# A four-layer graph network on one core: layer 2's mask codes loaded in half quarters, its elu split over ScalarE, GpSimd and VectorE

## The chip, the core and the metric

The kernel runs on one core of a Trainium2 chip. The metric is device time in microseconds (us) for one execution. The core's engines are called here as in the profile: PE (TensorE, matrix products; PEld is its weight load), DVE (VectorE), ACT (ScalarE), POOL (GpSimd) and SP (SyncE, which here only issues DMAs). Each engine runs its own instructions in order, and waits on semaphores for the others. SBUF is the on-chip memory with 128 partitions, PSUM the memory into which PE accumulates.

## The reference

4096 nodes with 256 features go through four layers, each of the form x = x + f(relu(layernorm(x)), adj) with one adjacency matrix of 4096 x 4096. Layer 0 is a graph attention with several gated branches, layer 1 a mean over neighbours, layer 3 a masked self attention. The change concerns layer 2 and the bias of layer 1:

```python
def _L1_gnn_ref(x, adj, W, b):
    a = (adj == 1).astype(x.dtype)
    deg = jnp.sum(a, axis=1, keepdims=True)
    agg = jnp.einsum('ij,jf->if', a, x) / deg
    return agg @ W.T + b

def _L2_gnn_ref(x, adj, W, a):
    ...
    h = x @ W
    e_src = h @ a[:D, 0]
    e_dst = h @ a[D:, 0]
    e = e_src[:, None] + e_dst[None, :]
    e = jnp.where(e > 0, e, NEG_SLOPE * e)
    att_logits = jnp.where(adj > 0, e, MASK_VAL)
    attention = jax.nn.softmax(att_logits, axis=1)
    h_prime = attention @ h
    return jax.nn.elu(h_prime)

h = jnp.maximum(_layernorm(x, axis=-1), 0.0)
x = x + _L1_gnn_ref(h, adj, L1_gnn_W, L1_gnn_b)
h = jnp.maximum(_layernorm(x, axis=-1), 0.0)
x = x + _L2_gnn_ref(h, adj, L2_gnn_W, L2_gnn_a)
```

## The kernel before

All rows of x stay in SBUF in the tile `xs`, as 32 row tiles of 128 rows by 256 features. Layer 0 has turned the adjacency matrix into a mask in bf16 (the "turned codes"), transposed so that the neighbour lies on the partition, and stored it in device memory as `codesT`: for each of 8 blocks of 4 row tiles, four quarters of 1 MB, a quarter holding 8 of the 32 chunks of 128 neighbours. In each partition a quarter is one run of 8 KB.

Layer 2 is an object of the class `Attention` (`att2`), which layer 0 uses too. It goes through the 8 blocks, and in each block through 16 pairs of chunks (128 pairs in all). For one pair:

- DVE computes two logits `y` (L354, one for each chunk, 128 x 512), from `ab_row` (the terms of the row nodes, spread over all partitions), `cdst` (the term of the neighbour) and `b` (a copy of half of `ab_row`, L352, made once a block).
- POOL subtracts the mask (L358, 128 x 1024, both chunks at once). The turned codes are its second operand.
- ACT takes the exponential of each chunk (L386), which also adds the neighbour's term.
- PE multiplies (L407): 4 row tiles by 2 chunks, each with 257 columns, the first column of ones giving the softmax's denominator. Four accumulators `acc` in PSUM collect the block; the pool has five.

There are 8 buffers for `y`, and PE is issued 3 pairs behind DVE.

The softmax needs a bound for each row, and that is what `reach` (L289 for a block's first chunk, L291 for the others) computes ahead: DVE keeps the running extreme `run` over all 32 chunks of a block, from the same turned codes. It runs 16 + 7 pairs ahead of the pairs that PE consumes (LEAD is 7), so during block b it finishes block b+1 and begins block b+2. When a block's run is complete, `top` follows in steps: PE transposes the run (L311), DVE reduces it and forms `ab` (L315 to L320), PE transposes `ab` (L323), ACT copies it and issues a DMA that stores it (`l_ab_d`, L340) and then one that loads it spread over all partitions (`ab_row`, L342). These two DMAs are on ACT's queue, among the exponentials. The next block's copy of `b` waits for `ab_row`.

The turned codes of layer 2 come through `stored` (L944 to L948): the first request for a quarter takes a buffer of the pool `l2_turned` and issues the load on SP. The pool has 8 buffers, two blocks' worth. So quarter q of block b+2 takes the buffer of quarter q of block b, and SP's issue waits until POOL's subtraction on the last pair of that quarter (pairs 3, 7, 11 and 15) has read it. The first of DVE's runs that needs the new quarter waits for the load. In blocks 0 to 5 codes for a later block are loaded; blocks 6 and 7 load nothing and have no runs of a block after next.

The order of instructions on each engine isn't the order of the program's text: the framework's scheduler moves them when the kernel is built, and places the runs of `reach` earlier than written, where it holds that their codes will have come. On the chip each engine follows that order.

At the end of a block `run` takes the reciprocals of the denominators (`rden`, L416), one for each row tile, and calls `finish2` (L953 to L970), which computes x + elu(h) for the block's four row tiles. With h = acc * rden, it uses elu(h) = max(h, 0) + min(exp(h), 1) - 1, written as max(h - 1, -1) + min(exp(h - 1 + 1), 1):

- `hp` = acc * rden - 1, row tiles 0 and 2 on ACT (L963, with `minus` as its bias), 1 and 3 on DVE (L959);
- `e` = exp(hp + 1), one operation of 128 x 1024 on ACT (L967);
- DVE: e = min(e, 1) + rows of x (L969), then rows = max(hp, -1) + e (L970), each 128 x 1024.

Layer 1 adds its bias `b1`, which `load_row` brings into SBUF spread over all partitions, through POOL's DMA queue, at the start of layer 1. POOL's queue at that place goes on with statistics of the layer norm (L117) and loads of adjacency (L173). Layer 2's first step is a layer norm of `xs`, which takes away any constant added to a row. Layer 3 follows layer 2 and reads `xs` row tile by row tile: statistics, layer norm, projections.

Of the kernel before, what the change touches and what calls it, by code (L numbers as in the profile page):

```python
# [11 lines left out]
F32 = mybir.dt.float32  # L12
# [9 lines left out]
P = 128  # L22
# [19 lines left out]
def kernel(ctx: ExitStack, tc: tile.TileContext, w: dict, out: bass.AP):  # L42
# [49 lines left out]
    def load_matrix(pool, name, eng=None):  # L92
        src = w[name]
        k, m = src.shape[0] // P, src.shape[1]
        t = pool.tile([P, k, m], F32, name=f"w_{name}")
        (eng or nc.gpsimd).dma_start(out=t, in_=src.rearrange("(k p) m -> p k m", p=P))
        return t
# [94 lines left out]
    class Attention:  # L192
        def __init__(self, es, tag, slope, lag, n_y, blocks, turned, finish, ps_top=None):
            self.tag, self.slope, self.lag, self.n_y = tag, slope, lag, n_y
            self.turned, self.finish = turned, finish

            self.links = []
            self.blocks = [{"at": at, "n": n} for at, n in blocks]
            vp = es.enter_context(tc.tile_pool(name=f"{tag}_sd", bufs=1))
            self.sdst = vp.tile([P, NT], F32, name="sdst")  # L200
            self.cdst = vp.tile([P, NT], F32, name="cdst")
            self.own_dst, self.held = None, False
            self.ab_d = [
                dram.tile([2, n, P], F32, name=f"{tag}_ab_d{k}") for k, (_, n) in enumerate(blocks)
            ]
            self.picks, self.spread = None, 0
            self.small = es.enter_context(tc.tile_pool(name=f"{tag}_small", bufs=4))
            self.row_p = es.enter_context(tc.tile_pool(name=f"{tag}_rows", bufs=2))
            self.ps_run = es.enter_context(tc.tile_pool(name=f"{tag}_run", bufs=1, space=PSUM))
            self.ps_top = ps_top or es.enter_context(  # L210
                tc.tile_pool(name=f"{tag}_top", bufs=1, space=PSUM)
            )
# [59 lines left out]
        def reach(self, n):  # L272

            b, c = n // PPB, n % PPB * 2
            st = self.blocks[b]
            at, n = st["at"], st["n"]
            if c == 0:
                st["run"] = self.ps_run.tile([P, RB, P], F32, tag="run", name="run")[:, 0:n, :]  # L280
            for j in range(c, c + 2):
                code = self.turned(b, j // QT)[:, :, j % QT, :]
                dst = self.dst_of(slice(j, j + 1))
                to = st["run"]
                if j == NT - 1:
                    to = self.row_p.tile([P, RB, P], F32, tag="run", name="run_sb", bufs=1)
                    to = to[:, 0:n, :]
                if j == 0:
                    nc.vector.tensor_scalar(to, code, dst, None, ALU.subtract)  # L289
                else:  # L290
                    nc.vector.scalar_tensor_tensor(  # L291
                        to, code, dst, st["run"], ALU.subtract, ALU.min
                    )
                st["run"] = to
            if c == NT - 2 and not self.held:
                self.links.append(self.top(b))
                if b == 0:
                    self.top_now()
# [48 lines left out]
        def logits(self, y, b, c, mask):  # L347

            st = self.blocks[b]
            if c == 0:  # L350
                st["b"] = self.ps_b.tile([P, RB, P], F32, tag="b", name="b")[:, 0 : st["n"], :]
                nc.vector.tensor_copy(st["b"], st["ab"][:, 1, :, :])  # L352
            for k in range(2):
                nc.vector.scalar_tensor_tensor(  # L354
                    y[:, :, k, :], st["ab"][:, 0, :, :], self.cdst[:, c + k : c + k + 1],
                    st["b"], ALU.add, ALU.max,
                )
            nc.gpsimd.tensor_tensor(y, y, mask[:, :, c % QT : c % QT + 2, :], ALU.subtract)  # L358

        def run(self, es, lead, n_acc, ahead=lambda n: None):  # L360

# [11 lines left out]
            for n in range(len(pairs) + LAG):  # L373
                if n < len(pairs):
                    b, c = pairs[n]
                    ahead(n)
                    if n + PPB + lead < len(pairs):
                        self.reach(n + PPB + lead)
                    y = self.y_p.tile([P, RB, 2, P], F32, tag="y", name="y")
                    ys[n] = y = y[:, 0 : self.blocks[b]["n"], :, :]  # L380
                    self.logits(y, b, c, self.turned(b, c // QT))
                if n >= LAG:
                    b, c = pairs[n - LAG]
                    y = ys.pop(n - LAG)
                    for k in range(2):
                        nc.scalar.activation(  # L386
                            y[:, :, k, :], y[:, :, k, :], AF.Exp,
                            bias=self.sdst[:, c + k : c + k + 1],
                        )
                    if c == 0:  # L390
                        accs[b] = [
                            ps_acc.tile([P, D + 1], F32, tag="acc", name="acc")
                            for _ in range(self.blocks[b]["n"])
                        ]


                    held.append((c, y))
                    edge = NT - 2 - c < 4 or b > 0 and c < 4
                    if edge and len(held) < 2:
                        self.link()  # L400
                        continue
                    terms = [(r, c1 + k, y1) for r in range(len(accs[b]))
                             for c1, y1 in held for k in range(2)]
                    if not edge:
                        terms.sort(key=lambda term: term[1])
                    for r, j, y1 in terms:
                        nc.tensor.matmul(  # L407
                            out=accs[b][r], lhsT=y1[:, r, j % 2, :], rhs=self.v[:, j, 0 : D + 1],
                            start=(j == 0), stop=(j == NT - 1),
                        )  # L410
                    held.clear()
                    if c == NT - 2:
                        done = accs.pop(b)
                        rden = self.small.tile([P, RB], F32, tag="rden", name="rden")
                        for r, acc in enumerate(done):
                            nc.vector.reciprocal(rden[:, r : r + 1], acc[:, 0:1])  # L416
                        self.finish(self.blocks[b]["at"], done, rden)
                self.link()
# [522 lines left out]
    l2 = ctx.enter_context(ExitStack())  # L941
    loaded = {}

    def stored(b, q):  # L944
        if (b, q) not in loaded:
            loaded[b, q] = turned_p.tile([P, RB, QT, P], BF16, tag="turned", name="turned")
            nc.sync.dma_start(out=loaded[b, q], in_=codesT[b][q])
        return loaded[b, q]  # L948

    minus = const.tile([P, 1], F32, name="minus")  # L950
    nc.gpsimd.memset(minus, -1.0)

    def finish2(at, accs, rden):  # L953

        h = work2.tile([P, RB, D], F32, tag="hp", name="hp")
        for r, acc in enumerate(accs):
            by = rden[:, r : r + 1]
            if r % 2:
                nc.vector.tensor_scalar(  # L959
                    h[:, r, :], acc[:, 1 : D + 1], by, -1.0, ALU.mult, ALU.add  # L960
                )
            else:
                nc.scalar.activation(  # L963
                    h[:, r, :], acc[:, 1 : D + 1], AF.Identity, scale=by, bias=minus
                )
        e = work2.tile([P, RB, D], F32, tag="e", name="e")
        nc.scalar.activation(e, h, AF.Exp, bias=ones[:, 0:1])  # L967
        rows = xs[:, at : at + RB, :]
        nc.vector.scalar_tensor_tensor(e, e, 1.0, rows, ALU.min, ALU.add)  # L969
        nc.vector.scalar_tensor_tensor(rows, h, -1.0, e, ALU.max, ALU.add)  # L970

    cuts2 = [(t, RB) for t in range(0, NT, RB)]
    att2 = Attention(l2, "l2", 0.01, 3, 8, cuts2, None, finish2)
# [19 lines left out]
    with ExitStack() as es:  # L993
# [3 lines left out]
        over_a = es.enter_context(tc.tile_pool(name="l1_a", bufs=AHEAD))  # L997
        vp = es.enter_context(tc.tile_pool(name="l1_v", bufs=1))
        w1 = load_matrix(vp, "L1_gnn_WT")
        b1 = load_row(vp, "L1_gnn_b")  # L1000
        late1 = vp.tile([P, NB - EARLY, BT, 2, D], F32R, name="late1")
        v1 = [t[:, b, :, :, :] for t in (early1[0], late1) for b in range(t.shape[1])]
        work = es.enter_context(tc.tile_pool(name="l1_work", bufs=2))
# [124 lines left out]

    with ExitStack() as es:
        att2.hold(es)  # L1130
        turned_p = es.enter_context(tc.tile_pool(name="l2_turned", bufs=8))
        work2 = es.enter_context(tc.tile_pool(name="l2_work", bufs=1))
        att2.turned, att2.held = stored, False
        with ExitStack() as ps_:
            pst = ps_.enter_context(tc.tile_pool(name="l2_pst", bufs=3, space=PSUM))
            psm = ps_.enter_context(tc.tile_pool(name="l2_psm", bufs=3, space=PSUM))
# [252 lines left out]
```

## Time and profile before

| | us |
|---|---|
| runs | 2970.71, 2976.31, 2978.07 |
| median | 2976.31 |
| the profiled execution | 2973.7 |
| its span in the profile | 2971.9 |
| granted PE clock, mean | 0.988 of full speed |

The profile is of one execution. Its page has the busy time of each engine, groups of instructions by line (busy time, mean of one in ns, idle time of the engine before them and what ended it), and the DMA issues. In the groups `out<-in` are the program's names of tiles. Layer 2's pairs run from 1509.28 to 1999.08 us of the span; layer 1 begins at about 1200, layer 3's matmuls over the scores at 2043.69. Some rows that the reader needs:

| line, engine | what | mean of one |
|---|---|---|
| L354, DVE | logits y, 128x512 | 0.74 us (one starts 0.66 after the one before) |
| L291, DVE | run, 128x512 | 0.75 us (0.79 apart when one needs the one before) |
| L358, POOL | mask, 128x1024 | 2.16 us (2.10 apart) |
| L386, ACT | exponential, 128x512 | 0.71 us |
| L963, ACT | hp of one row tile | 0.56 us |
| L967, ACT | e, 128x1024 | 1.15 us |
| L959, DVE | hp of one row tile | 0.48 us |
| L969, DVE | e, 128x1024 | 1.22 us (last block) to 1.71 |
| L970, DVE | rows, 128x1024 | 1.22 us (last block) to 2.49 |
| L947, SP | load of a quarter, 1 MB, 8 KB runs | 4.8 us from issue to landing (median) |

A duration is from an instruction's start to its end; the engines overlap one instruction's end with the next one's start, so the distance between starts is what a chain of them costs. Where an engine idles, the profile names the event that ended the wait; a wait for several things is put down to the one that came last.

### The profile page before, as it was taken

The numbers are of one execution on the slowest core, as the hardware profiler recorded it, in microseconds if no ns is written. First come the engines' busy times: TensorE is split into PE (matmuls) and PEld (weight loads), VectorE is DVE, ScalarE is ACT, GpSimd is POOL, SyncE is SP. The second block draws the span as 40 slices with busy tenths as digits, with TensorE's granted clock in tenths as the row PEclk, the third lists the DMA queues.
The fourth block names the chain that finished last, engine by engine and source line by source line (L and its number), as shares of the span: only waits on it lengthen the run. The fifth ranks groups of instructions, "written<-read, shape, count | busy, mean of one in ns | idle before, by whom it ended". The sixth has DMA issues, their size and how long they took to land.

```text
span 2971.9 us, 35206 instructions
## 1 busy us (share of the span) xinstructions
PE 2864.4 (96%) x13381; PEld 2336.5 (79%) x13381; DVE 1901.4 (64%) x3475; ACT 1262.0 (42%) x1929; POOL 952.2 (32%) x718
## 2 busy tenths in 40 slices
PE   7999999999999999899999999999999999999999
PEld 6888888856555666788778777888888888888888
DVE  6987767345555554577688888656766666566653
ACT  6765555389995333881354333343111112111111
POOL 5676665545554333320055555550000000000000
PEclk9999999999999999999999999999999999999999
DMA  6966664154551000785432212002111111111100
GB/s 155 235 141 142 133 125 127 43 87 77 78 77 34 8 8 15 190 226 156 140 129 79 75 68 78 29 14 87 37 62 36 38 36 60 40 34 63 34 8 8
DMA packets 109161, 238.62 MB, mean 80 GB/s; under 512 B 10736, under 2 KB 31200, under 8 KB 100288
## 3 DMA queue, kind: packets, MB, share of 16 engines
q1 hardware_dynamic: 68496, 159.34, 15.5%
q0 software_dynamic: 37696, 69.11, 15.1%
q10 hardware_dynamic: 2800, 7.92, 0.7%
q8 instruction: 105, 1.72, 0.2%
q14 instruction: 64, 0.52, 0.1%
HBM read 265.63 MB, written 37.81 MB: 102 GB/s over the span
## 4 chain that ended last, share of the span: by engine, by line
PE 64%; DVE 9%; ACT 8%; POOL 7%; issue 6%; DMA 6%; POOLq 0%; ACTq 0%; DVEq 0%
PE acc L1321 15%; PE s L154 15%; PE acc L407 13%; PE mm L154 9%; PE acc L1052 8%; POOL y L358 5%; ACT sign L180 3%; DVE y L354 3%; DVE run L291 3%; DMA turned<-codesT 2%; DMA ab_row<-l_ab_d 1%; DMA a<-in_adj_dram 1%; PE q_ps L154 1%; DMA l_ab_d<-abT_sb 1%; PE cT L530 1%
## 5 line engine op out<-in xcount | busy, mean ns | idle before, releaser
L407 PE MATMUL acc<-v,y 128*128 128x257 f32 x4096 | 930.2, 386 | 12.3 <-ACT hp L963 4.9
L407 PEld LDWEIGHTS acc<-v,y 128*128 128x128 f32 x4096 | 778.1, 192 | 126.5 <-ACT hp L963 6.5
L358 POOL TENSOR_TENSOR y<-y,turned 128x1024 f32<-128x1024 f32 (+1 forms) x272 | 549.1, 2039 | 323.8 <-DVE y L354 222.3
L386 ACT ACTIVATE y<-y,sdst 128x512 f32<-128x512 f32 (+1 forms) x544 | 350.3, 690 | 417.8 <-POOL y L358 417.6
L1321 PE MATMUL acc<-v,y 128*128 128x257 f32 x2048 | 454.5, 380 | 0.4 <-DVE rden L1329 0.4
L154 PE MATMUL s<-qT,hT 128*128 128x256 f32 x2048 | 445.2, 379 | 0.7 <-ACT qT L1269 0.7
L1314 ACT ACTIVATE y<-y 128x1024 f32<-128x1024 f32 x128 | 132.2, 1055 | 714.3 <-DVE y L1313 710.0
L154 PEld LDWEIGHTS s<-qT,hT 128*128 128x128 f32 x2048 | 389.0, 190 | 54.2 <-ACT qT L1269 1.4
L1321 PEld LDWEIGHTS acc<-v,y 128*128 128x128 f32 x2048 | 387.1, 190 | 55.9 <-issue 0.8
L354 DVE SCALAR_TENSOR_TENSOR y<-ab_row,cdst,b 128x512 f32<-128x512 f32 (+1 forms) x544 | 366.2, 709 | 62.9 <-PE acc L407 61.0
L180 ACT ACTIVATE sign<-a,limits 128x1024 bf16<-128x1024 bf16 x256 | 293.8, 1148 | 22.1 <-DMA a<-in_adj_dram 16.8
L1283 DVE SCALAR_TENSOR_TENSOR y<-code,s 128x512 f32<-128x512 bf16 x256 | 175.9, 688 | 100.9 <-PE s L154 100.6
L291 DVE SCALAR_TENSOR_TENSOR run<-turned,v,run 128x512 f32<-128x512 bf16 (+1 forms) x270 | 186.4, 690 | 63.9 <-ACT turned L535 55.6
L291 DVE SCALAR_TENSOR_TENSOR run<-turned,dst,run 128x512 f32<-128x512 bf16 x240 | 180.5, 752 | 33.1 <-DMA turned<-codesT 29.6
L1313 DVE TENSOR_TENSOR y<-y,top 128x1024 f32<-128x1024 f32 x128 | 146.2, 1215 | 43.0 <-PE top L1307 43.0
L1290 DVE TENSOR_TENSOR mx<-mx,y 128x512 f32<-128x512 f32 x224 | 154.8, 691 | 7.4
L535 ACT ACTIVATE turned<-cT,log_wide 128x1024 bf16<-128x1024 bf16 x128 | 139.0, 1104 | 39.8 <-PE cT L530 31.5
L154 PE MATMUL mm<-kept 128*128 128x512 f32 x288 | 136.7, 615 | 3.0 <-ACT sz L840 1.9
L173 POOL DMA_DIRECT2D a<-in_adj_dram x128 | 76.6, 600 | 196.3 <-ACT sign L180 141.1
L1052 PE MATMUL acc<-early,eq 128*128 128x512 f32 x512 | 128.7, 401 | 2.5 <-DVE early L456 2.2
L1052 PE MATMUL acc<-late,eq 128*128 128x512 f32 x512 | 122.6, 391 | 0.0
L1052 PEld LDWEIGHTS acc<-early,eq 128*128 128x128 f32 x512 | 96.8, 191 | 26.8 <-DVE early L456 2.4
(234 smaller groups left out, 3005.5 us busy)
## 6 DMA issues: line engine op xcount, KB each, us to landing
turned<-codesT SPq DMA_DIRECT2D x36, 1024.0 KB, 4.9
adj_t<-in_adj_dram POOLq DMA_DIRECT2D x128, 256.0 KB, 6.1
codesT<-turned SPq DMA_DIRECT2D x32, 1024.0 KB, 4.9
a<-in_adj_dram POOLq DMA_DIRECT2D x128, 256.0 KB, 4.7
code<-codesT SPq DMA_DIRECT2D x128, 256.0 KB, 4.8
code<-codesT SPq DMA_DIRECT2D x64, 512.0 KB, 7.1
ab_row<-l_ab_d ACTq DMA_DIRECT2D x14, 512.0 KB, 3.8
xs<-in_x_dram SPq DMA_DIRECT2D x8, 512.0 KB, 13.4
```

The costliest lines, as they stand in the source:

```text
L154: nc.tensor.matmul(out=ps, lhsT=lhsT_of(k), rhs=rhs_of(k), start=(k == 0), stop=(k == n - 1))
L180: nc.scalar.activation(sign, self.came[g], AF.Sign, bias=limits[:, v : v + 1], accum_out=over[:, t, v, q : q + 1],)
L291: nc.vector.scalar_tensor_tensor(to, code, dst, st["run"], ALU.subtract, ALU.min)
L354: nc.vector.scalar_tensor_tensor(y[:, :, k, :], st["ab"][:, 0, :, :], self.cdst[:, c + k : c + k + 1], st["b"], ALU.add, ALU.max,)
L358: nc.gpsimd.tensor_tensor(y, y, mask[:, :, c % QT : c % QT + 2, :], ALU.subtract)
L386: nc.scalar.activation(y[:, :, k, :], y[:, :, k, :], AF.Exp, bias=self.sdst[:, c + k : c + k + 1],)
L407: nc.tensor.matmul(out=accs[b][r], lhsT=y1[:, r, j % 2, :], rhs=self.v[:, j, 0 : D + 1], start=(j == 0), stop=(j == NT - 1),)
L1052: nc.tensor.matmul(out=acc, lhsT=eqs[c // (NT // 2)][:, ts(c % (NT // 2), P)], rhs=v1[c // BT][:, c % BT, :, :], start=(c == 0), stop=(c = ...
L1283: nc.vector.scalar_tensor_tensor(y[:, :, c : c + 2, :], st["code"][:, :, c : c + 2, :], -BIG / UNIT, ps, ALU.mult, ALU.add,)
L1290: nc.vector.tensor_tensor(mx, mx, y[:, :, c : c + 2, :], ALU.max)
L1313: nc.vector.tensor_tensor(part, part, top, ALU.subtract)
L1321: nc.tensor.matmul(out=accs[r], lhsT=st["y"][:, r, c, :], rhs=v3[:, c, :], start=(c == 0), stop=(c == NT - 1),)
```

## The change

Three things are changed together.

- Layer 2's turned codes are loaded in half quarters: 4 chunks (two pairs), 512 KB, in each partition 4 runs of 1 KB. The pool has 16 buffers of half the size, so the same memory. `per` (chunks in one load) takes the place of `QT` in the class; in layer 0 it stays QT. There are 64 loads on SP for 32. A half's buffer comes free after POOL's subtraction on its second pair.
- `finish2` computes elu(h) + x as relu(h) + min(exp(h), 1) + (x - 1). On ACT two operations for each row tile, straight from PSUM: relu(acc * rden) to `h` and exp(acc * rden) to `e`. Then POOL adds `h` to the rows (128 x 1024), and one DVE operation gives rows = min(e, 1) + rows. In the last block POOL isn't used: DVE does both, one row tile at a time.
- The rows hold x - 1 during layer 2: POOL subtracts 1 from layer 1's bias right after its load. The tile `minus` goes.

```diff
--- before.py
+++ after.py
@@ -193,6 +193,7 @@
         def __init__(self, es, tag, slope, lag, n_y, blocks, turned, finish, ps_top=None):
             self.tag, self.slope, self.lag, self.n_y = tag, slope, lag, n_y
             self.turned, self.finish = turned, finish
+            self.per = QT
 
             self.links = []
             self.blocks = [{"at": at, "n": n} for at, n in blocks]
@@ -279,7 +280,7 @@
             if c == 0:
                 st["run"] = self.ps_run.tile([P, RB, P], F32, tag="run", name="run")[:, 0:n, :]
             for j in range(c, c + 2):
-                code = self.turned(b, j // QT)[:, :, j % QT, :]
+                code = self.turned(b, j // self.per)[:, :, j % self.per, :]
                 dst = self.dst_of(slice(j, j + 1))
                 to = st["run"]
                 if j == NT - 1:
@@ -355,7 +356,8 @@
                     y[:, :, k, :], st["ab"][:, 0, :, :], self.cdst[:, c + k : c + k + 1],
                     st["b"], ALU.add, ALU.max,
                 )
-            nc.gpsimd.tensor_tensor(y, y, mask[:, :, c % QT : c % QT + 2, :], ALU.subtract)
+            at = c % self.per
+            nc.gpsimd.tensor_tensor(y, y, mask[:, :, at : at + 2, :], ALU.subtract)
 
         def run(self, es, lead, n_acc, ahead=lambda n: None):
 
@@ -378,7 +380,7 @@
                         self.reach(n + PPB + lead)
                     y = self.y_p.tile([P, RB, 2, P], F32, tag="y", name="y")
                     ys[n] = y = y[:, 0 : self.blocks[b]["n"], :, :]
-                    self.logits(y, b, c, self.turned(b, c // QT))
+                    self.logits(y, b, c, self.turned(b, c // self.per))
                 if n >= LAG:
                     b, c = pairs[n - LAG]
                     y = ys.pop(n - LAG)
@@ -941,33 +943,33 @@
     l2 = ctx.enter_context(ExitStack())
     loaded = {}
 
-    def stored(b, q):
-        if (b, q) not in loaded:
-            loaded[b, q] = turned_p.tile([P, RB, QT, P], BF16, tag="turned", name="turned")
-            nc.sync.dma_start(out=loaded[b, q], in_=codesT[b][q])
-        return loaded[b, q]
-
-    minus = const.tile([P, 1], F32, name="minus")
-    nc.gpsimd.memset(minus, -1.0)
+    HT = QT // 2
+
+    def stored(b, u):
+        if (b, u) not in loaded:
+            loaded[b, u] = turned_p.tile([P, RB, HT, P], BF16, tag="turned", name="turned")
+            nc.sync.dma_start(out=loaded[b, u], in_=codesT[b][u // 2][:, :, ts(u % 2, HT), :])
+        return loaded[b, u]
 
     def finish2(at, accs, rden):
 
         h = work2.tile([P, RB, D], F32, tag="hp", name="hp")
+        e = work2.tile([P, RB, D], F32, tag="e", name="e")
         for r, acc in enumerate(accs):
-            by = rden[:, r : r + 1]
-            if r % 2:
-                nc.vector.tensor_scalar(
-                    h[:, r, :], acc[:, 1 : D + 1], by, -1.0, ALU.mult, ALU.add
-                )
-            else:
+            for to, func in ((h, AF.Relu), (e, AF.Exp)):
                 nc.scalar.activation(
-                    h[:, r, :], acc[:, 1 : D + 1], AF.Identity, scale=by, bias=minus
-                )
-        e = work2.tile([P, RB, D], F32, tag="e", name="e")
-        nc.scalar.activation(e, h, AF.Exp, bias=ones[:, 0:1])
+                    to[:, r, :], acc[:, 1 : D + 1], func, scale=rden[:, r : r + 1]
+                )
+        if at == NT - RB:
+
+            for r in range(RB):
+                row = xs[:, at + r, :]
+                nc.vector.tensor_tensor(row, row, h[:, r, :], ALU.add)
+                nc.vector.scalar_tensor_tensor(row, e[:, r, :], 1.0, row, ALU.min, ALU.add)
+            return
         rows = xs[:, at : at + RB, :]
-        nc.vector.scalar_tensor_tensor(e, e, 1.0, rows, ALU.min, ALU.add)
-        nc.vector.scalar_tensor_tensor(rows, h, -1.0, e, ALU.max, ALU.add)
+        nc.gpsimd.tensor_tensor(rows, rows, h, ALU.add)
+        nc.vector.scalar_tensor_tensor(rows, e, 1.0, rows, ALU.min, ALU.add)
 
     cuts2 = [(t, RB) for t in range(0, NT, RB)]
     att2 = Attention(l2, "l2", 0.01, 3, 8, cuts2, None, finish2)
@@ -997,7 +999,9 @@
         over_a = es.enter_context(tc.tile_pool(name="l1_a", bufs=AHEAD))
         vp = es.enter_context(tc.tile_pool(name="l1_v", bufs=1))
         w1 = load_matrix(vp, "L1_gnn_WT")
+
         b1 = load_row(vp, "L1_gnn_b")
+        nc.gpsimd.tensor_scalar(b1, b1, -1.0, None, ALU.add)
         late1 = vp.tile([P, NB - EARLY, BT, 2, D], F32R, name="late1")
         v1 = [t[:, b, :, :, :] for t in (early1[0], late1) for b in range(t.shape[1])]
         work = es.enter_context(tc.tile_pool(name="l1_work", bufs=2))
@@ -1128,9 +1132,9 @@
 
     with ExitStack() as es:
         att2.hold(es)
-        turned_p = es.enter_context(tc.tile_pool(name="l2_turned", bufs=8))
+        turned_p = es.enter_context(tc.tile_pool(name="l2_turned", bufs=16))
         work2 = es.enter_context(tc.tile_pool(name="l2_work", bufs=1))
-        att2.turned, att2.held = stored, False
+        att2.turned, att2.per, att2.held = stored, HT, False
         with ExitStack() as ps_:
             pst = ps_.enter_context(tc.tile_pool(name="l2_pst", bufs=3, space=PSUM))
             psm = ps_.enter_context(tc.tile_pool(name="l2_psm", bufs=3, space=PSUM))
```

Lines after L291 shift by one or more in the changed kernel: L354 becomes L355, L358 L360, L416 L418, L947 L951; the new ones are L960 (ACT), L967 and L968 (DVE, last block), L971 (POOL), L972 (DVE) and L1004 (POOL, the bias).

More of the change, by code (lines that the diff above doesn't have):

```diff
@@ L942 @@
     loaded = {}
-    def stored(b, q):
-        if (b, q) not in loaded:
-            loaded[b, q] = turned_p.tile([P, RB, QT, P], BF16, tag="turned", name="turned")
-            nc.sync.dma_start(out=loaded[b, q], in_=codesT[b][q])
-        return loaded[b, q]
-    minus = const.tile([P, 1], F32, name="minus")
-    nc.gpsimd.memset(minus, -1.0)
+    HT = QT // 2
[4 more added lines that the diff above has]
+        return loaded[b, u]
     def finish2(at, accs, rden):
         h = work2.tile([P, RB, D], F32, tag="hp", name="hp")
+        e = work2.tile([P, RB, D], F32, tag="e", name="e")
         for r, acc in enumerate(accs):
-            by = rden[:, r : r + 1]
-            if r % 2:
-                nc.vector.tensor_scalar(
-                    h[:, r, :], acc[:, 1 : D + 1], by, -1.0, ALU.mult, ALU.add
-                )
-            else:
-                nc.scalar.activation(
-                    h[:, r, :], acc[:, 1 : D + 1], AF.Identity, scale=by, bias=minus
-                )
-        e = work2.tile([P, RB, D], F32, tag="e", name="e")
-        nc.scalar.activation(e, h, AF.Exp, bias=ones[:, 0:1])
+            for to, func in ((h, AF.Relu), (e, AF.Exp)):
+                nc.scalar.activation(
+                    to[:, r, :], acc[:, 1 : D + 1], func, scale=rden[:, r : r + 1]
+                )
+        if at == NT - RB:
[4 more added lines that the diff above has]
+            return
         rows = xs[:, at : at + RB, :]
-        nc.vector.scalar_tensor_tensor(e, e, 1.0, rows, ALU.min, ALU.add)
-        nc.vector.scalar_tensor_tensor(rows, h, -1.0, e, ALU.max, ALU.add)
+        nc.gpsimd.tensor_tensor(rows, rows, h, ALU.add)
+        nc.vector.scalar_tensor_tensor(rows, e, 1.0, rows, ALU.min, ALU.add)
     cuts2 = [(t, RB) for t in range(0, NT, RB)]
```

## The prediction

> **What bounds the kernel now.** The profiled execution took 2973.7 us (span 2971.9). I read the page's groups first: TensorE carries 96%, and in layer 2 its work is L407.
>
> ```profile
> PE 2864.4 (96%) x13381; PEld 2336.5 (79%) x13381; DVE 1901.4 (64%) x3475; ACT 1262.0 (42%) x1929; POOL 952.2 (32%) x718
> L291 DVE SCALAR_TENSOR_TENSOR run<-turned,dst,run 128x512 f32<-128x512 bf16 x240 | 180.5, 752 | 33.1 <-DMA turned<-codesT 29.6
> ```
>
> Layer 2's 2048 matmul records of L407 run from 1509.28 to 1999.08, 489.8 us. A stretch without idle time has one record each 0.2175 us, so 445.4 plus some 4 us of transposes is PE's own need, and about 40 us of the layer are PE waiting. The table of windows shows where (columns: window, its length, busy time of PE, PEld, DVE, ACT, POOL, granted clock, DMA share, GB/s).
>
> ```profile
> 1509.00:1566.00 57.00, 56.72 (x256) 49.34 (x257) 49.84 (x76) 26.35 (x41) 40.78 (x20) 0.97 0.24 85
> 1692.00:1757.00 65.00, 59.44 (x264) 50.77 (x263) 52.18 (x78) 23.12 (x36) 34.20 (x17) 0.95 0.20 69
> 1757.00:1823.00 66.00, 59.38 (x266) 50.79 (x264) 52.18 (x78) 24.56 (x38) 35.77 (x17) 0.95 0.21 80
> 1884.00:1938.00 54.00, 54.00 (x254) 47.20 (x253) 30.46 (x49) 24.10 (x39) 35.24 (x18) 1.00 0.03 11
> ```
>
> The first block and the last two, which load nothing, are PE's; the middle ones take 65 us where PE needs some 56.5. There DVE is busy 52 of 65 us and never waits for PE. What ends its waits, in the layer's window:
>
> ```profile
> DVE run L291 <- DMA turned<-codesT: 29.6, 12, 5.0
> DVE b L352 <- DMA ab_row<-l_ab_d: 18.8, 7, 8.5
> DVE run L289 <- DMA turned<-codesT: 18.8, 5, 4.2
> PE abT L323 <- DVE ab L320: 21.1, 5, 4.9
> ```
>
> PE stands at abT because DVE is late with ab. The chain of waits through one middle block shows the loop (start, length, what):
>
> ```profile
> 1688.91 4.72 DMA turned<-codesT
> 1693.67 0.05 issue
> 1693.72 0.75 DVE run L289
> ...
> 1702.32 3.12 POOL y L358
> 1705.46 4.80 DMA turned<-codesT
> 1710.35 0.77 DVE run L291
> ...
> 1716.14 2.14 POOL y L358
> 1718.30 4.64 DMA turned<-codesT
> 1723.03 0.77 DVE run L291
> ```
>
> GpSimd's L358 on a quarter's last pair frees the buffer, SP loads into it, and DVE's next run, in order, waits for that load. So the middle of layer 2 is DVE's own work plus this round trip, four times a block. The copies of b (L352) mark the blocks: 1503.5, 1553.4, 1613.4, 1677.5, 1743.1, 1808.1, 1873.5; intervals 49.9, 60.1, 64.1, 65.6, 65.0, 65.4.
>
> **Half quarters.** A half is freed by GpSimd on pair 2u+1 and not only on pair 4q+3. But DVE's order is fixed when the kernel is built, and there the runs (j0 to j31 of the block after next) move forward to meet the earlier loads: in a middle block j0 still stands behind y4, j8 now stands ahead of y6, j16 ahead of y11, j20 ahead of y13, j28 right behind y15. Each half's run thus follows closely on the y that frees its buffer. I step one middle block from its b copy (time 0) by rows of this trace: one y instruction 0.66 us, two a pair; a run 0.79 behind a run; GpSimd starts 1.65 after a pair's first y and takes 2.10 each.
>
> The load from the end of GpSimd's subtraction to DVE's start costs 4.9 to 5.0 now (1688.88 to 1693.72). No 512 KB load of turned codes with 1 KB runs is in the trace. Nearest is xt, of that size and run length; ab_row, also 512 KB, took 3.6 at its least:
>
> ```profile
> turned<-codesT SPq DMA_DIRECT2D x36, 1024.0 KB, 4.9
> ab_row<-l_ab_d ACTq DMA_DIRECT2D x14, 512.0 KB, 3.8
> xt<-in_x_dram SPq DMA_DIRECT2D x8, 512.0 KB, 4.0
> ```
>
> I take 4.2 (5.0 less 0.8 for 4.8 to 4.0); bounds 3.8 (ab_row's best) and 5.0 (nothing saved).
>
> y0 to y4 end at 7.2, but y1 leaves GpSimd at 6.5, so j0 starts at 10.7: wait 3.5. j0 to j2, y5, j3, j4 to j7, three rden: 18.7. j8 needs y5 off GpSimd (16.8) plus 4.2: 21.0, wait 2.3. Through y7 24.5; the new L972 waits for the GpSimd add (25.5) and ends at 27.0. Behind it stand j9 to j11, y8, y9 (GpSimd waits for these two): 32.0; j12, freed by y7: 33.9, wait 1.9. j16, by y9: 39.4, wait 1.0. j20, by y11: 48.2, wait 3.0. ab at about 56.5; j24, by y13: wait 1.1. y15 starts at 59.3, leaves GpSimd at 63.0, so j28 starts at 67.2, wait 5.0. The next b copy stands behind it and needs y15's exponentials and two DMAs on ScalarE's queue, 11.2 us from GpSimd's start on y15 (now 1731.87 to 1743.10): 72.2. Waits add to some 20 us, against 13.1 now (4.0, 0.55, 1.5, 4.9, 1.9). A run that follows a y goes at 0.66, so I take 1 us off: period 71.
>
> Before this sets in, block 0 gains: its j0 need not wait until 1519.86 and b copies at about 1550.7 (2.7 earlier). Block 1, stepped in the same way, waits 2.9 for rden and 1.7 for L972 and ends at about 1616.3, 2.9 later than now. Then four intervals of 71 stand in the place of 260.1: +23.9. Blocks 6 and 7 load nothing and stay PE's. With 3.8 a load, six waits on the path shrink by 0.4: 68.6, 9.6 us less in all; with 5.0, 19 more. SP has 32 more issues of 0.32 us, nothing against its 369 us of waiting for L358.
>
> The Trainium skill's "DMA: Bandwidth & Descriptors", section "Rules for kernel authors", asks for 1 MiB or more a DMA, which speaks against halves; its "Latency and other measured facts" puts some 2 us of a DMA down as fixed. By that, 4.8 would become 3.4 (an estimate from that page), and the whole sum about 14 us less than mine; xt's 4.0 decides for me.
>
> **The finish.** Removed from DVE a block: two hp of 0.48, L969 1.71, L970 2.49 (GpSimd beside it; 1.22 each in the last block): 5.2. Added: one L972, 1.2 to 1.7. The 3.5 us gained is in the stepping above, and goes into the next wait for a load. ScalarE does 8 operations of about 0.55 (L963: 0.556) in place of 2 and an exponential of 1.15: 4.4 for 2.3, on an engine that waits 257.8 us for GpSimd. Its row r3 gates the GpSimd add (2.36, as L907), which delays y6 and y7 there and with them j12: counted. The accumulators come free after two ScalarE operations, 1.1 us, where it was 0.5: in the middle PE has slack before abT; in blocks 6 and 7 bounds are 0 and 2 us, I take 0.5.
>
> The Trainium skill's "Perfetto Trace Analysis", section "Optimizing Scalar/DVE Operations", warns that GpSimd and DVE share an SBUF read port, so that moving work between them may not help. L970's 2.49 against 1.22 agrees. By the rule the add would stretch what DVE runs beside it: if it doubled the four y instructions of 0.66, 2.6 a block, most of it spent in L972's wait anyway.
>
> The last block's finish, per row on DVE, is 8 short operations of 0.42 to 0.48, the early rows beside PE's end: behind the last row about 2.5 us less than now (e, L969, L970: 2000.07 to 2004.35). Part of that is PE's gain at layer 3's start: -1.5 (bounds 0, -2.5).
>
> **The bias row.** L1004 makes GpSimd wait for b1, issued at 1201.55 and landing 11.1 us later, with L117's statistics (now 1210.68) and the load of adjacency behind it; it takes about 1.2 (L666). The statistics come some 3 us later; behind them wait DVE's hT copies and PE. The a loads have slack. Bounds 0 and +3.2; I take +0.5, since PE at that start waits for several others. `minus` is a memset less: nothing.
>
> **Sum.** 2.9 + 23.9 + 0.5 - 1.5 + 0.5 = +26.3; the stepping counts every wait at its full length, so I round down to +24: 2973.7 + 24 = 2998. The median of the runs, 2976.3, is 2.6 above the profiled one; I keep 2998.
>
> **Rivals.** (1) *The loads become shorter than their neighbours*, 3.2 from GpSimd to DVE: six waits of 1.0 less, period about 65, 2974, no change. For: halves carry half the bytes. Against: xt at 3.8 to 5.4. Chance 0.16. (2) *The waits go away and layer 2 becomes PE's*: if DVE's runs find their halves loaded, the middle blocks fall to 52.2 - 3.5 of DVE plus the 8 us of ab_row and rden that stay, 57 to 60 a block: four at 59 in the place of 260 give -24, with the tail 2948; the bound is the 40 us of idle PE, 2936. It decides from the point where four y's of DVE stand between freeing pair and run; the built order has one or two. Chance 0.18. (3) *The start of layer 1 pays in full* and block 1 loses more: 3003 to 3010; in the forecast's range. Forecast (2980 to 3016, its own range): 0.66.
>
> Within 0.3%, 9 us, nothing can be told from no change: 2967 to 2985. From the cases: faster 0.18, same 0.15, slower 0.67. The range for 8 in 10 reaches down to part of the second rival: 2952 to 3016.
>
> **What would show it.** Right: b copies some 70 us apart from the third block on; waits of DVE for turned codes up from 48.4 to 90 us or more, their number from 17 to 40 or more; PE's idle at abT up from 21 us. Landing of the halves at 4.0. DVE's busy time 3.5 us less a block. Wrong, if halves land in under 3.4, or if b copies stand 60 us apart. Layer 1's start moves by less than 3 us.

## The result, and the profile after

| | median, us | runs | ratio to the kernel before, 95% interval |
|---|---|---|---|
| before | 2976.9 | 2970.7 to 2978.1 | |
| changed | 2993.7 | 2992.2 to 3000.7 | 1.0058, 1.0040 to 1.0077 |

The change makes the kernel slower by 0.6%. The profiled execution's span is 2991.8 us (2971.9 before), with the granted clock at 0.987 (0.988). Layer 2's matmuls take 506.6 us from first to last (490.0 before). The copies of b stand at 1507.0, 1553.8, 1614.4, 1684.1, 1755.7, 1824.5, 1893.4 and 1947.1 us, so 46.8, 60.6, 69.7, 71.7, 68.8, 68.9 and 53.6 apart: the four middle blocks average 69.8 where they took 65.0.

The table of windows of the changed kernel (window, length, busy time of PE, PEld, DVE, ACT, POOL, clock, DMA share, GB/s), a middle block on each of the first two lines and one without loads on the third:

```profile
1684.00:1756.00 72.00, 58.45 (x264) 50.05 (x264) 51.98 (x76) 24.62 (x41) 37.06 (x17) 0.93 0.21 66
1756.00:1825.00 69.00, 57.97 (x256) 49.41 (x255) 51.92 (x76) 24.63 (x41) 37.08 (x17) 0.93 0.21 69
1893.00:1947.00 54.00, 54.00 (x253) 47.20 (x253) 29.14 (x44) 24.28 (x41) 36.05 (x17) 1.00 0.03 10
```

DVE is as busy in a middle block as before (52 us) although the new elu has one pass over the rows where there were two: the 3.5 us that it was to save are not there. All the added length is DVE waiting. The waits of layer 2's window in the changed kernel (engine, line, what it waited for, us in total, times, longest):

```profile
DVE run L292 <- DMA turned<-codesT: 50.3, 23, 4.7
...
PE abT L324 <- DVE ab L321: 40.2, 5, 11.0
POOL xs L971 <- ACT hp L960: 27.3, 6, 5.9
...
DVE run L290 <- DMA turned<-codesT: 14.9, 5, 4.0
...
DVE b L353 <- DMA ab_row<-l_ab_d: 13.4, 7, 8.9
DVE xs L972 <- POOL xs L971: 13.1, 7, 4.2
```

DVE waits 65.2 us for turned codes (48.4 before), 28 times (17), and 13.1 us for the add on POOL, which is new. PE's wait for `ab` went from 21.1 to 40.2. These are the kinds of waits that the prediction described. But they don't say which of the parts brought them, and that is where the experiments went against it.

The timeline of one middle block around the new finish (start, us, engine, line, operation; in brackets the idle time before and what ended it):

```profile
1706.67 0.47 ACT L960 ACTIVATE hp<-acc,rden 128x256 f32<-128x256 f32 x1 [2.33 <-DVE rden L418]
...
1707.23 2.35 POOL L971 TENSOR_TENSOR xs<-xs,hp 128x1024 f32<-128x1024 f32 x1 [5.70 <-ACT hp L960]
1709.54 5.18 POOL L360 TENSOR_TENSOR y<-y,turned 128x1024 f32<-128x1024 f32 x2
1709.61 3.12 DVE L972 SCALAR_TENSOR_TENSOR xs<-e,xs 128x1024 f32<-128x1024 f32 x1 [1.01 <-POOL xs L971]
...
1714.75 0.52 SPq L951 DMA_DIRECT2D turned<-codesT  x1
```

The add stands in POOL's queue ahead of the mask of y6 and waits there for ScalarE's last relu. The masks of y6 and y7 start some 2 us later for it: DVE is done with y6 at 1707.30, and the mask of y6 starts at 1709.54. Then DVE's pass and the masks run side by side and slow each other: 3.12 us for the pass and 5.18 for two masks, which take 4.2 elsewhere. Only then is the half of y7 free and its load issued (1714.75).

### The profile page after: what moved, and what is told of

Same layout as the page of the kernel before. It is cut to its first block, busy times and chain, and to the rows that moved or that the text cites. A ratio compares the mean times of both kernels' runs of the same rounds, so it can differ in the third digit from the quotient of the medians.

```text
span 2991.8 us, 35303 instructions
## 1 busy us (share of the span) xinstructions
PE 2863.7 (96%) x13381; PEld 2335.9 (78%) x13381; DVE 1896.5 (63%) x3458; ACT 1269.5 (42%) x1969; POOL 968.1 (32%) x725
## 4 chain that ended last, share of the span: by engine, by line
PE 64%; ACT 8%; DVE 8%; POOL 7%; issue 6%; DMA 6%; SPq 0%; POOLq 0%; DVEq 0%; ACTq 0%
PE acc L409 15%; PE acc L1325 15%; PE s L154 15%; PE mm L154 8%; PE acc L1056 8%; POOL y L360 4%; ACT sign L180 4%; DVE run L292 3%; DVE y L355 2%; DMA turned<-codesT 2%; DMA ab_row<-l_ab_d 1%; DMA a<-in_adj_dram 1%; PE cT L532 1%; PE q_ps L154 1%; ACT t L747 1%
## 5 line engine op out<-in xcount | busy, mean ns | idle before, releaser
L360 POOL TENSOR_TENSOR y<-y,turned 128x1024 f32<-128x1024 f32 (+1 forms) x272 | 548.8, 2036 | 298.9 <-DVE y L355 227.3
L355 DVE SCALAR_TENSOR_TENSOR y<-ab_row,cdst,b 128x512 f32<-128x512 f32 (+1 forms) x544 | 365.2, 709 | 64.3 <-PE acc L409 59.4
L154 PE MATMUL mm<-kept,zT 128*128 128x256 f32 x512 | 114.8, 380 | 0.5 <-ACT zT L758 0.5
```

The source lines that it names most:

```text
L154: nc.tensor.matmul(out=ps, lhsT=lhsT_of(k), rhs=rhs_of(k), start=(k == 0), stop=(k == n - 1))
L355: nc.vector.scalar_tensor_tensor(y[:, :, k, :], st["ab"][:, 0, :, :], self.cdst[:, c + k : c + k + 1], st["b"], ALU.add, ALU.max,)
L360: nc.gpsimd.tensor_tensor(y, y, mask[:, :, at : at + 2, :], ALU.subtract)
```

## The experiments

Theory 1 was the prediction's: the loss is DVE's order with half quarters. Theory 2 was its rival: the elu loses the time.

**Each part alone.** First, the changed kernel with the old `finish2` and the old bias, so half quarters alone (the bodies, as before and as changed, are left out here):

```diff
+    minus = const.tile([P, 1], F32, name="minus")
+    nc.gpsimd.memset(minus, -1.0)
...
-        nc.gpsimd.tensor_scalar(b1, b1, -1.0, None, ALU.add)
...
```

> Half-quarter loads with 16 buffers alone; the elu and layer 1's bias are as before. Theory 1 (the loss is DVE's order: runs of reach moved close behind the y that frees their half, so that DVE waits for a load 7 times a block): the loss is all here, and DVE has about 3.5 us more work a block than in the changed kernel: copies of b 70 to 73 us apart in the middle, 2990 to 3005. Theory 2 (the loss is the elu: eight ScalarE operations a block and GpSimd's add in the queue of masks): no loss here, 2970 to 2980, copies 65 apart.

Measured: 2967.5 us, ratio 0.9961 (0.9946 to 0.9975). Theory 1's 2990 to 3005 is clearly missed, and theory 2's "no loss" is on the right side: the halves alone make the kernel a little *faster*. Middle blocks 60.1, 64.5, 65.1 and 63.1. DVE's waits for turned codes in this kernel:

```profile
DVE run L292 <- DMA turned<-codesT: 23.2, 12, 4.4
...
DVE run L290 <- DMA turned<-codesT: 14.4, 5, 4.4
```

They fell to 37.6 us, from 48.4. Second, the kernel before with the new `finish2` and the new bias, so whole quarters and 8 buffers:

```diff
-    minus = const.tile([P, 1], F32, name="minus")
-    nc.gpsimd.memset(minus, -1.0)
...
+        nc.gpsimd.tensor_scalar(b1, b1, -1.0, None, ALU.add)
...
```

> The new elu and the bias less 1 alone; turned codes in whole quarters with 8 buffers, as before. Theory 1: no loss; DVE has 3.5 us less a block, of which the four middle blocks keep between 0 and 3.5 each: 2960 to 2977. Theory 2: the loss is here, 2987 to 3000.

Measured: 2989.4 us, ratio 1.0043 (1.0029 to 1.0056): theory 2. Middle blocks 68.1, 67.4, 67.8 and 68.0, with no half quarter in the kernel:

```profile
DVE run L291 <- DMA turned<-codesT: 44.3, 14, 5.2
...
DVE run L289 <- DMA turned<-codesT: 18.9, 5, 4.1
...
DVE xs L968 <- POOL xs L967: 14.0, 7, 5.0
```

Here the elu alone raises the waits for codes from 48.4 to 63.2 us and adds 14.0 for POOL. So the loss is the elu's, though a good part of it is paid at the loads. The wait of j8 (the run of chunk 8 of the block after next) shows how. It stands behind y9 in both kernels, and its quarter comes free with the mask of y7. In the second middle block that mask ends 29.8 us after the copy of b, where it was 27.9, and j8 waits 2.8 us in each middle block where it waited at most 0.6.

**Holding DVE's order.** The other half of theory 1 can be tried apart from that: that these waits come from the place of the runs in DVE's order. A run may issue only behind the y of a given pair, so that the scheduler can't bring it further forward; this is an order on DVE alone, without a wait.

```diff
+            self.last[b * PPB + c // 2] = last.ins
...
-                        self.reach(n + PPB + lead)
+                        if self.back is None or n < self.back:
+                            self.reach(n + PPB + lead)
+                        else:
+                            with tc.issue_after(self.last[n - self.back]):
+                                self.reach(n + PPB + lead)
...
+        att2.back = 3
         att2.run(es, LEAD, 5)
```

> The changed kernel, with DVE's order held: the runs of a pair may issue at most three pairs of y earlier than the program's text has them, so j0 stands behind y6 or later and j28 behind four pairs of the next block; loads, buffers and elu as in the changed kernel. Theory 1: DVE's waits for turned codes fall from 65 us to under 15, PE idle at abT goes, the middle blocks come to 57 to 61 us, 2940 to 2960: faster than both. Theory 3 (the 64 smaller loads cost by themselves, by their issues on SP or their landing): waits stay over 40 us and the time stays at 2985 to 2995.

Measured: 2956.9 us, ratio 0.9927 (0.9908 to 0.9947); middle blocks 60.2, 60.0, 60.3 and 60.5. DVE's waits for turned codes fell from 65.2 to 1.6 us, and these are now the waits (columns as above):

```profile
DVE b L354 <- DMA ab_row<-l_ab_d: 47.6, 7, 8.8
...
DVE xs L978 <- POOL xs L977: 13.3, 7, 3.4
```

PE's wait for ab is 12.4 us. The wait of b for `ab_row` has grown by 34 us, and yet the kernel is faster: DVE now reaches b early. The 64 smaller loads are not a cost by themselves (theory 3). The same was done to the kernel before, with `att2.back = 2`:

> The kernel before, with DVE's order held in the same way at two pairs; quarters, 8 buffers and the old elu. Quarter q is freed by y of pair 4q+3 and its first run then stands behind pair 4q+7: three pairs of y between them. Theory 1: waits for turned codes fall from 48 us to under 25, middle blocks 58 to 63 us, 2945 to 2968. If the gain needs the halves: 2970 to 2980, as before.

Measured: 2946.9 us, ratio 0.9894 (0.9876 to 0.9912), at the low end of theory 1's range and below the held changed kernel. Layer 2's matmuls take 458.2 us, where PE needs some 449.

**The four combinations, held.** Half quarters with the old elu, held at three pairs:

> Half quarters and 16 buffers with the old elu and bias, and DVE's order held at three pairs as in the held changed kernel (2956.9). If the elu costs some 10 us by itself even where DVE waits for no load: 2943 to 2950. If it lost only through loads that came late: as there, 2953 to 2960.

Measured: 2946.9 us, 0.9887 (0.9863 to 0.9910). And whole quarters with the new elu, held at two:

> Whole quarters and 8 buffers with the new elu and bias, order held at two pairs as in the held kernel before (2946.9). If the elu costs by itself where DVE waits for no load: 2953 to 2962. If the difference between the two held kernels is the halves': 2944 to 2950.

Measured: 2962.1 us, 0.9932 (0.9910 to 0.9953), at the upper end of what was expected if the elu costs by itself. Together (ratios to the kernel before):

| | quarters | halves |
|---|---|---|
| old elu, order as built | 1 | 0.9961 |
| new elu, order as built | 1.0043 | 1.0058 |
| old elu, held | 0.9894 | 0.9887 |
| new elu, held | 0.9932 | 0.9927 |

Held, the halves give nothing, and the elu costs 0.4%. The quarters were held at two pairs and the halves at three; a further run (below) has the changed kernel at five, with 2958.3 us for 2956.9, so the distance matters little. As built, the halves win 0.4% with the old elu and, within the intervals, nothing with the new one: the two parts alone, -10 and +12 us, don't add to the +17 of both.

**What in the elu costs.** Theory 4: POOL's add in the queue of the masks, and DVE's pass beside it. Theory 5: ScalarE's eight operations. The changed kernel with the last block's finish in every block:

```diff
-        if at == NT - RB:
+        if True:
```

> The changed kernel, but every block's finish is done as the last one's: for each row tile two operations on DVE, nothing on GpSimd; ScalarE's eight operations, the half quarters and the bias stay. Theory 4 (the elu loses because GpSimd's add stands in the queue of the masks, waits there for ScalarE's last relu and holds y6 and y7, and so the release of their codes, by 2.3 us, and because DVE's single pass takes 3.1 us beside GpSimd): most of the loss of 17 us goes, 2962 to 2977. Theory 5 (the eight ScalarE operations lose it: exponentials and accumulators later): no change, 2987 to 2997.

Measured: 2968.8 us, 0.9960 (0.9944 to 0.9976): as good as the halves with the old elu, though ScalarE does its eight operations and DVE eight short ones. That speaks for theory 4. In the next run the add and the pass are held until POOL has masked pair 9 of the next block (`masked` is that subtraction):

```diff
+            if c // 2 == 9:
+                with tc.issue_after(masked.ins):
+                    while self.later:
+                        self.later.pop()()
...
-        nc.gpsimd.tensor_tensor(rows, rows, h, ALU.add)
-        nc.vector.scalar_tensor_tensor(rows, e, 1.0, rows, ALU.min, ALU.add)
+
+        def add_up():
+            nc.gpsimd.tensor_tensor(rows, rows, h, ALU.add)
+            nc.vector.scalar_tensor_tensor(rows, e, 1.0, rows, ALU.min, ALU.add)
+
+        att2.later.append(add_up)
```

> The changed kernel, with GpSimd's add and DVE's pass over the rows held until GpSimd has masked pair 9 of the next block; all else as changed. Theory 4: y6 and y7 are masked 2.3 us earlier, but a later mask is held for as long, so part of the loss goes: 2970 to 2988. Theory 5: no change, 2987 to 2997.

Measured: 2981.3 us, 1.0009 (0.9995 to 1.0023), so most of the loss goes. The group of DVE's passes in this kernel against the changed one (busy us, mean ns, idle before):

```profile
L979 DVE SCALAR_TENSOR_TENSOR xs<-e,xs 128x1024 f32<-128x1024 f32 x7 | 8.6, 1225 | 14.2 <-POOL xs L978 14.2
```

```profile
L972 DVE SCALAR_TENSOR_TENSOR xs<-e,xs 128x1024 f32<-128x1024 f32 x7 | 21.9, 3130 | 13.1 <-POOL xs L971 13.1
```

The same operation takes 1.225 us where POOL happens to be idle and 3.130 where it masks. The wait for the add stays. So the last two experiments on this leave the add where it was and move the pass alone, behind DVE's y of pair 9 (theory 6). In the held changed kernel:

```diff
-        nc.vector.scalar_tensor_tensor(rows, e, 1.0, rows, ALU.min, ALU.add)
+        att2.later.append(
+            lambda: nc.vector.scalar_tensor_tensor(rows, e, 1.0, rows, ALU.min, ALU.add)
+        )
```

> The held changed kernel (2956.9), with DVE's pass over the rows moved behind pair 9 of the next block; GpSimd's add stays where it was, the rest too. Theory 6 (the held elu loses its 10 us on DVE: a wait of 2 us for GpSimd's add and a pass of 3.1 us beside GpSimd's mask, 5.1 a block for the old two passes' 3.6): 2944 to 2950. Theory 4 alone (the add in the queue of the masks): stays at 2953 to 2960.

Measured: 2946.2 us, 0.9886 (0.9865 to 0.9908). The elu's cost in the held order is gone, with its add still in the queue of the masks. The passes in this kernel:

```profile
L984 DVE SCALAR_TENSOR_TENSOR xs<-e,xs 128x1024 f32<-128x1024 f32 x7 | 17.2, 2457 | 0.0
```

No wait is left before them (13.3 us over seven passes in the held changed kernel), and a pass still takes 2.46 us beside POOL, for 3.13: of 2.6 us less a block the wait is 1.9. So by these rows the larger part of the cost was that the pass stood in DVE's queue, ahead of the y's, before its add was there; the wait and the longer pass were not tried apart. The same edit in the changed kernel with nothing held:

> The changed kernel with DVE's pass over the rows moved behind pair 9 of the next block, and nothing held: GpSimd's add and the runs stay where the scheduler puts them. If the pass (its wait of 1 us or more and its 3.1 us beside the masks) is what turns the halves' gain into a loss, by putting DVE and the masks behind it late: 2965 to 2980, within the halves alone (2967.5) and before. If the loss is the add in the queue of the masks: 2985 to 2995, as changed.

Measured: 2973.4 us, 0.9986 (0.9975 to 0.9998), in the range expected if the pass decides, and out of the one for the add in the queue of the masks; middle blocks 64.5, 63.7, 65.3 and 64.1. That one edit takes back 0.7% where the change had lost 0.6%; to the halves alone 0.25% are left. DVE's waits for codes stay high (63.7 us), so they aren't by themselves the measure of the loss. The passes in this kernel:

```profile
L984 DVE SCALAR_TENSOR_TENSOR xs<-e,xs 128x1024 f32<-128x1024 f32 x7 | 12.6, 1799 | 0.0
```

With the wait before them, the seven passes cost DVE 35.0 us in the changed kernel, 22.8 with add and pass late, and 12.6 here: 12 and 22 us less. By the ratios, the two runs gained some 15 and 21 us. The sizes agree, which supports the pass as the cause; it is no proof, since only the middle blocks are bound by DVE. Moving the pass also lets y8 and y9 go ahead of the run that waits for y7's half; the run doesn't tell these two apart. And where nothing is held, the scheduler places the runs anew in each kernel. In the middle blocks j16 stands behind y10 in the changed kernel, and behind y11 or y12 with the halves alone, with the add on DVE, with the add late and here. So these runs change more than their edit says; the held ones leave the scheduler less room.

**Two that came otherwise.** The held changed kernel with every finish on DVE:

> The held changed kernel, with the finish of every block on DVE, one row tile at a time (as in the run with the add on DVE, 2968.8, but held); half quarters. Theories 4 and 6: no GpSimd in it, 2943 to 2950. Theory 5 (ScalarE's eight operations): 2953 to 2960.

Measured: 2951.4 us, 0.9912 (0.9893 to 0.9931), between the two expectations. DVE waits 13.5 us for ScalarE's relu there, so ScalarE's operations may not be wholly free once the loads are; but the interval overlaps that of the old elu, held (0.9863 to 0.9910). And the changed kernel held at five pairs in place of three:

> The changed kernel held at five pairs in the place of three: j0 right behind y5 and two pairs nearer to the subtraction that frees its codes. Theory 1 in its new form (DVE's waits for loads come from how few pairs the built order leaves between the freeing y and the run): waits for turned codes between 5 and 45 us and the time between the two, 2960 to 2985. If holding helps by something else: 2953 to 2960.

Measured: 2958.3 us, 0.9925 (0.9897 to 0.9953), with 1.9 us of waits for turned codes: a miss for theory 1's dose: both numbers lie where they were expected if holding helps by something else. The waits for codes are gone here too, so the run doesn't speak against them as the cause; it shows that five pairs are already enough to clear them. No point between this and the order as built was measured.

## Why the prediction was right or wrong

The time was forecast at 2998 and came at 2993.7, with the sign right. The first block came as stepped (46.8 us for 47.2), and so did the middle ones (69.8 for 71); the second did not (60.6 for 65.6): the wait of 2.9 us for `rden` that was stepped there, the larger part of the miss, didn't occur. In the block from 1684.1 the waits stepped and found, in order: j0 3.5 and 4.0; j8 2.3 and 2.0; the pass 1.0 and 1.0; j12 1.9 and 0.9; j16 1.0 and 3.4; j20 3.0 and 2.5; j24 1.1 and none; j28 5.0 and 4.6; b 2.0 and 0.6. They add to 20.8 and 19.0 us (the five waits that the prediction lists for the kernel before add to 12.9, not 13.1). A walk of one in-order engine through the built order, with durations of the trace, was good to 2% in the middle blocks. Part of that is luck: the pass took 1.6 us more than stepped and j16 waited 2.4 us longer (its load took 5.35 us), while j12, j24 and b together waited 3.5 us less. In the sum, too, errors partly cancel: blocks 0 and 1 together came 5.5 us under it and the middle ones 4.9, while the start of layer 2, put at nothing, took 3.1 us more.

So DVE's waits for loads in the built order were the right mechanism of the time, but the part of the change that they were put down to was wrong. These steps failed or were off:

- **"Half quarters", the term of 2.9 + 23.9.** The walk was made over the order of the whole change, with the add and the pass in it, and its sum was put down to the halves. Alone they measure -10 us (2967.5 against 2977.8). The walk could not have shown this: with the old elu the scheduler gives another order. In its middle blocks j16 stands behind y11 or y12 and waits at most 1.2 us (behind y10 in the changed kernel, with 1.6 to 3.4), j20 waits nowhere (2.5 us a block in the changed kernel), and DVE waits 37.6 us for codes in the place of 65.2. (The prediction's "j0 still stands behind y4" fits the changed kernel; in the kernel before it is y5.)
- **"The 3.5 us gained".** L972 was put at 1.2 to 1.7 us, the range of L969's row, whose lower end is the last block, where POOL is idle; it took 3.13 in seven blocks of seven, plus a wait of 1.0 in a middle block (13.1 us over seven). So a middle block of DVE saved some 1.0 us of 5.2 (4.1 spent), and the elu alone measures +12 us (2989.4 against 2977.8). The rows to price it were at hand: L970's 2.49 with POOL at work was quoted and not used.
- **The rule on shared ports.** The Trainium skill's "Perfetto Trace Analysis", section "Optimizing Scalar/DVE Operations", warns of moving work between DVE and GpSimd for their shared SBUF read port. The prediction looked for this in the y's beside the add and let the wait absorb it. The runs agree with the rule, but for another pair: the three y's that begin at 1706.56, most of them beside the add, took 2.04 us, so 0.66 apart as elsewhere, while the pass took 1.225 us alone and 3.130 beside a mask.
- **The load of a half** was put at 4.0 from issue to landing; the median is 3.7 (3.6 at the least). The estimate from the skill's page, 3.4, and xt's 4.0 are equally far off. The lower bound leaned on ab_row's least time, which is 3.3 and not 3.6. The same skill asks for 1 MiB or more a DMA where bandwidth is the aim ("DMA: Bandwidth & Descriptors", "Rules for kernel authors"); no loss from smaller loads shows here: halves alone were faster as built, and equal when held.
- **The accumulators, the last block, the bias.** PE's wait for accumulators went from 4.9 and 2.3 us (ScalarE and DVE) to 6.0. The last block was to bring -1.5; from layer 2's last matmul to the end of the span it is 972.3 where it was 972.6, so -0.3. The bias was to cost 0.5. Its operation took 0.86 us, and the statistics behind it came at 1213.86 for 1210.68, later as stepped; but layer 1, from its first comparison of codes to its last, takes 253.1 (253.2 before), so it cost nothing that shows. It was not run alone.
- **Not foreseen:** layer 2's start is 3.1 us longer, from the first ab to the first copy of b (29.9 for 26.8; 30.0 with the halves alone, 26.7 with the elu alone). It isn't the halves by themselves: with the add late, which has them too and the same order of runs there, it is 27.1. In the changed kernel DVE waits twice for PE's transposes there, 3.6 us in all; with the add late it waits once, 1.1. Why stays open.
- **What would show it:** 40 waits and 90 us for codes were asked for; there were 28 and 65.2. The steps themselves gave seven waits for codes in each of four blocks, so 28, with 17.8 us a block, and the list was not counted from them.

The rival "the waits go away and layer 2 becomes PE's" was priced at 2936 to 2948 and given the wrong condition: it needs no half quarters at all. Held, the kernel before reaches 2946.9, with whole quarters.

What stays open: why the halves win as built with the old elu and nothing with the new one (the scheduler's order differs, as said above, and order and elu were not separated), and what share of the unheld loss is the pass's wait and what the order of y8 and y9 behind it. The fastest measured are three at 2946 to 2947, 1.1% under the kernel before: quarters or halves with the old elu, held, and the changed kernel held with its pass late. They can't be told apart.

## What to carry to other kernels

When several edits come together, step them apart: a walk through the order of the whole change gives the time and says nothing about which edit owns it. Price an operation by its row beside the neighbours that it will have, and look at what stands behind it on its queue: an add on an engine with time to spare and a pass that waits for it cost more than the two passes that they replaced. And where a scheduler brings work forward to meet a load, some ordering edges that hold it back can be worth more than smaller loads or less work.

## What the runs showed of the hardware

A load of a half quarter occupies SP's queue for 0.518 us where a whole quarter took 0.320 (medians of 64 and of 32 issues), although it moves half the bytes; in each partition it has four runs of 1 KB and not one of 8 KB. And the collision between DVE and POOL reaches tiny operations: in the changed kernel `ab`, 128 x 4, took 2.1 us in five blocks beside a mask, where it takes 0.15 alone. The kernel before has the like on a neighbouring operation (`m`, L317, 1.66 us in the middle blocks). One of the five:

```profile
L320 DVE TENSOR_TENSOR ab<-v,m 128x4 f32<-128x4 f32 x1 | 2.1, 2087 | 0.0
```

This one started at 1740.86, 0.05 us after a mask, and ended at 1742.95, 0.02 us after that mask's end. That is what it would look like if the short operation had waited until the mask was over; no run tests it apart.
